# A GCN layer and a graph attention layer on one core: the turned data's write-outs on another queue, one fetch placed later, the attention products' PSUM banks exchanged

## The chip, the cores and the metric

The kernel runs on one core of a Trainium2 chip. The metric is the time of one execution in device microseconds, as the median of several runs; smaller is better. The kernel before has a median of 2262.29 us over three runs, from 2256.73 to 2267.03. One further execution was profiled; all times of single steps come from it.

## What is computed

The input x has 128 elements (b) of 128 nodes by 512 features, all float32, and one 128 by 128 adjacency matrix. Cut to what matters:

```
h = relu(layernorm(x));  x = x + norm_adj @ (h @ W0) + b0
h = relu(layernorm(x));  q, k, v = h @ Wq + bq, h @ Wk + bk, h @ Wv + bv     (8 heads of 64)
attn = softmax(q k^T / 8 + (1 - adj) * -1e9);  x = x + (attn @ v) @ Wo + bo
```

## The kernel before

**Groups and slots.** The 128 elements are 32 groups (NG) of four (GB). One pass of the outer loop, a slot t, works on three groups at once: the W block multiplies group t+1 by the GCN weight, the blocks Q, K and V make q, k and v of group t, and the Y block multiplies the attention output of group t-1 by Wo. Each of these five products is a fast (Strassen-like, seven products, with a second level inside) multiplication of seven steps, so the places in a slot are called W0 to W6, Q0 to Q6, K0 to K6, V0 to V6 and Y0 to Y6; a "b" or "c" behind a place is a point after the first or second part of that step.

**The order is written by hand.** `at(slot, place, f, ...)` puts a function into a table, and `block` calls what stands at a place before it issues that step's products. Every engine executes its instructions in the order in which these calls issue them, so a place decides the position in each engine's queue. All DMAs of the kernel before are issued by SyncE (SP) and stand in one queue; SyncE waits at the head of its queue until what the next DMA needs is there. Eight semaphores are given to the DMAs in turn, so that a DMA also waits until the one issued eight before it has landed.

**Turning data through DRAM.** The attention weights of an element (128 queries by 8 heads by 128 keys) have to be transposed before they can be multiplied by v. `flip_att(g, b)` transposes blocks of 32 by 32 on VectorE (L917) and writes the 512 KB to a scratch tensor in DRAM (`turned<-att`, L918); `turn_att(g, b)` fetches them from there with the blocks exchanged, in four DMAs of 128 KB whose runs are 128 bytes long (`att<-turned`, L789, through `from_dram`). The normalised input of the attention layer takes the same way: `flip_h` (L776) and its write (`turned_h`, L778), and `turn_h` with `op_h<-turned_h` (L789). The first and the last group transpose on TensorE instead, in whole or in part.

**Where these steps stand in a slot of the middle** (group g = t-1; a minus means the slot before):

| element | exponentials and softmax end | flip and write | fetch |
|---|---|---|---|
| 0 | V and Y block of the slot before | Y6c of the slot before | W3 |
| 1 | Y block of the slot before | Q0b | Q2b |
| 2 | Y block of the slot before | Q2c | K0 |
| 3 | Y5 of the slot before to W2 | Q4b | K0b |

**The products.** `attend(g, b)` at V0 multiplies the turned weights of element b by v: 16 products on TensorE (L943), then a copy of the result by ScalarE into the operand of the Wo product (L407). The order of the elements is 2, 0, 1, 3. Elements 2 and 3 use the two small PSUM banks (`po`), element 0 uses bank b, element 1 that one of the banks a0 and a1 which the last step of k has used. Right before, VectorE still adds up k from bank b and that bank a (L481, L496); right behind come the scores of the next group (L868, in the order 0, 1, 3, 2), those of element 1 into bank b and the same bank a.

**Weights.** The weights don't fit into SBUF together. Each product's combined weight (40 slots, five parts of eight) is fetched anew in every slot, in five DMAs of 512 KB (`reload_w`, L1133), as soon as the product before it in the same buffer has read its part. `reloads_of` lists the places: those under "Q" fetch v (into q's buffer), under "K" fetch o, under "V" fetch q, under "Y" fetch k. v's second part stands at Q6c, and the products that last read its place in the buffer are those of Q6.

**Other steps that count below.** ScalarE reads q and k from PSUM (L811, L814), takes the statistics of the group that comes in (L340, L341), normalises (L372) and copies the mixed operands (L407, `op_a<-pa`); GpSimd works out the scale from the statistics (L349 to L354).

Of the kernel before, what the change touches and what calls it, by code (L numbers as in the profile page):

```python
# [97 lines left out]
def kernel(  # L98
# [16 lines left out]
    nc = tc.nc  # L115
# [6 lines left out]
    NG = B // GB  # L122
# [21 lines left out]
    def small_bank(name):  # L144
        return ps_t.tile([P, 512], F32, tag="bank", name=name)
# [4 lines left out]
    bank = {k: ps_c.tile([P, 512], F32, tag=f"bank_{k}", name=f"bank_{k}") for k in ("a0", "a1", "d0", "d1", "b", "c")}  # L150
    turn = [0]
# [7 lines left out]
    att_dram = [dp.tile([P, H * P], F32, tag=f"turned_{b}", name=f"turned_{b}") for b in range(GB)]  # L159
    h_dram = [dp.tile([P, H * P], F32, tag=f"turned_h_{y}", name=f"turned_h_{y}") for y in range(2)]  # L160
# [609 lines left out]
    def flip_h(g, b):  # L770

        half, j = divmod(b, 2)
        h2 = hs.pop((g, b)).rearrange("n (c i f) -> n c i f", c=NC, i=4)
        t = op_att.t[:, SLOTS - 12 : SLOTS - 4, :] if half else att_of(g - 2, 2 if g > 2 else 1)
        t = t.rearrange("p s n -> p (s n)")
        nc.vector.transpose(t.rearrange("n (i c j f) -> n j c i f", i=4, c=NC, j=2)[:, j], h2)  # L776
        if j:
            nc.sync.dma_start(h_dram[half], t)  # L778

    def turn_h(g, half):  # L780
        op_h[g] = op_norm
        first = LEFT_AT[S1 if half else A11]
        from_dram(op_norm.t[:, first : first + 8, :], h_dram[half])
# [46 lines left out]

    maxima, sums = {}, {}

    def att_of(g, b):


        return att_buf[(b if g == 0 else b + 4 - 2 * g) % (GB + 1)]

    def by_blocks(g, b):  # L840

        return 0 < g < NG - 1 and not turned_in_place(g, b)

    def weights_of(g, b):

        return att_of(g, b - 1 if 0 < g < NG - 1 else b)

    def turned(g, b):

        if turned_in_place(g, b):  # L850
            return weights_of(g, b)
        return att_of(g, b - 2 if g else b - 1)

    def turned_in_place(g, b):

        return g == NG - 1 or g == 0 and b >= 2
# [55 lines left out]
    def flip_att(g, b):  # L912

        t = turned(g, b).rearrange("q h k -> q (h k)")
        order = "q h (i k) -> q h i k" if by_blocks(g, b) else "q h (k i) -> q h i k"
        dst = t.rearrange("q (i h k) -> q h i k", i=4, h=H)
        nc.vector.transpose(dst, weights_of(g, b).rearrange(order, i=4))  # L917
        nc.sync.dma_start(att_dram[b], t)  # L918

    def turn_att(g, b):  # L920
        from_dram(turned(g, b), att_dram[b])
# [10 lines left out]
    def attend(g, b):  # L932
        if g not in op_o:
            op_o[g] = op_norm if g == NG - 1 else op_att
        aT = turned(g, b)
        if b == 2 or b == 3:
            po = small_bank(f"po_{g}_{b}")
        else:
            po = bank["b" if b == 0 else f"a{1 - turn[0]}"]
        for c in range(NC):  # L940
            for p in range(2):
                h = 2 * c + p
                nc.tensor.matmul(  # L943
                    po[p * HD : (p + 1) * HD, c * P : (c + 1) * P],
                    vs[g][:, b, h * HD : (h + 1) * HD],
                    aT[:, p * NC + c, :],
                    start=True,
                    stop=True,
                )
        op_o[g].fill(nc.scalar.copy, b, po)  # L950
# [18 lines left out]
    def at(slot, place, f, *args):  # L969
        plan.setdefault((slot, place), []).append((f, *args))  # L970

    for t in range(-1, NG + 1):


        last = t == NG - 1
        if 0 <= t - 1 < NG - 1:
            g = t - 1

            for first, final, place, f, *args in (
                ("W4", "-Y6c", "W1c" if t == 2 else "-Y6c", flip_att, 0),  # L980
                ("W6", "Q2", "W4" if t == 2 else "W3", turn_att, 0),
                ("Q4c", "Q1c", "Q0b", flip_att, 1),
                ("Q6", "Q3", "Q2b", turn_att, 1),
                ("W6", "-Y3", "-Y3", exponentials, 2, 0, H // 2),
                ("Q3c", "-Y4", "-Y4", exponentials, 2, H // 2, H),
                ("Q6b", "-Y5b", "W0c" if t == 2 else "-Y5b", softmax_end, 2),
                ("K0c", "-Y5", "-Y5", exponentials, 3, 0, H // 2),
                ("K1c", "-Y6", "-Y6", exponentials, 3, H // 2, H),
                ("K3c", "W0", "W2", softmax_end, 3),
                ("K1", "Q2c", "Q2c", flip_att, 2),  # L990
                ("K3", "Q4", "K0", turn_att, 2),
                ("K3", "Q3c", "Q4b", flip_att, 3),
                ("K5", "Q5", "K0b", turn_att, 3),
            ):
                place = first if t == 1 else final if last else place
                if f in (flip_att, turn_att) and turned_in_place(g, args[0]):
                    continue
                at(t - place.startswith("-"), place.strip("-"), f, g, *args)
            if t == 1:
                at(1, "K4", transpose_att, g, 2)  # L1000
                at(1, "K6", transpose_att, g, 3)
            for b in (2, 0, 1, 3):
                at(t, "V0", attend, g, b)
        if t == 0:

            at(0, "Q0b", ln2, 1, 0)
            at(0, "Q1b", ln2, 1, 1)
            at(0, "K6", norm_h, 1, 0)
            at(0, "K6", norm_h, 1, 1)
            at(0, "V4", transpose_h, 1, 0)  # L1010
            at(0, "V4", norm_h, 1, 2)
            at(0, "V5", transpose_h, 1, 1)
            at(0, "V5", norm_h, 1, 3)
            at(1, "W0", transpose_h, 1, 2)
            at(1, "W1", transpose_h, 1, 3)
            at(1, "W1b", attention_operands, 1)
            at(2, "Q5", attention_residual, 1, 0)
            at(2, "K1", attention_residual, 1, 1)
        elif 1 <= t + 1 < NG and t >= 0:
            g = t + 1  # L1020
            at(t, "Q3b" if g < NG - 1 else "Q0b", ln2, g, 0)
            at(t, "K0b" if g < NG - 1 else "Q3b", ln2, g, 1)
            if g == NG - 1:

                places = ("Q3", "Q4", "Q5", "Q5", "Q6", "Q6", "K1", "K2", "K2")
                steps = ((norm_h, 0), (norm_h, 1), (transpose_h, 0), (norm_h, 2), (transpose_h, 1), (norm_h, 3))
                steps += ((transpose_h, 2), (transpose_h, 3))
            else:
                places = ("K1c", "K2c", "K4c", "K5b", "K3", "K4b", "K6b", "K6b", "Y6b")
                if t == 1:  # L1030
                    places = ("K2c", "K3c", "K6", "K6b", "K4b", "K5b", "V0b", "V0b", "Y6b")
                steps = ((norm_h, 0), (norm_h, 1), (norm_h, 2), (norm_h, 3))
                steps += tuple((flip_h, b) for b in range(GB))
                for half in range(2):
                    at(t, ("V3", "Y0")[half], turn_h, g, half)
            for place, (f, b) in zip(places, steps):
                at(t, place, f, g, b)
            at(t, places[8], attention_operands, g)
            at(t + 1, "Q3", attention_residual, g, 0)
            at(t + 1, "Q4", attention_residual, g, 1)  # L1040
# [3 lines left out]
        if 3 <= t + 2 < NG:  # L1044
            place = (t - 1, "Y6b") if t > 1 else (t, "W0")
            at(*place, load_x, t + 2, (0,), t > 1)
            at(*place, load_x, t + 2, (1,), t > 1)
        if 2 <= t + 2 < NG:
            g = t + 2
# [13 lines left out]
        if 0 <= t < NG:  # L1063
            g = t
# [30 lines left out]
        if last:  # L1095
            g = t
# [38 lines left out]
    def reloads_of(t):  # L1135

        when = {
            "Q": ((t, "Q2"), (t, "Q6c"), (t, "K1"), (t, "K1"), (t, "K3")),
            "K": ((t, "K5"), (t, "V0c"), (t, "V0c"), (t, "V0c"), (t, "V0c")),
            "V": ((t, "V3"), (t, "Y0"), (t, "Y0"), (t, "Y0"), (t, "Y3")),  # L1140
            "Y": ((t, "Y4"), (t + 1, "W2"), (t + 1, "W4"), (t + 1, "Q1"), (t + 1, "Q1")),
        }
        if t + 1 == NG - 1:

            when["Y"] = ((t, "V2"),) * len(PARTS)
        elif t == NG - 1:

            when["Q"] = ((t, "K3"),) * len(PARTS)
        if t == 1:

            when["Q"] = ((1, "K4"),) * len(PARTS)
            when["K"] = ((1, "V0c"),) * len(PARTS)
        for kind in "QKVY":
            if kind in "QKV" and t == NG:
                continue
            reading[0] += 1
            for part, place in enumerate(when[kind]):
                at(*place, reload_w, reading[0] + 2, part)
# [159 lines left out]
```

## Time and profile before

| quantity | value |
|---|---|
| median of three runs | 2262.29 us (2256.73 to 2267.03) |
| the profiled execution, its own time | 2243.55 us |
| its span, first to last instruction | 2241.8 us |
| TensorE busy | 2200.8 us, 98% of the span |
| VectorE, GpSimd, ScalarE busy | 1884.1, 1868.6, 1285.5 us |
| DMA: bytes moved, mean rate | 599.23 MB, 267 GB/s |
| packets under 512 bytes | 765664 of 908108 |
| `turned<-att`: DMAs, median time from issue to landing | 122 of 512 KB, 5.2 us |
| `att<-turned`: the same | 488 of 128 KB, 4.0 us |

How to read it: the busy share of an engine says how much of the span it has work; the view of waits says what an engine that had none was waiting for. The timeline gives, for each group of instructions, the start, the length, the engine, the line, what it writes and reads, the count, and in brackets the idle time before it with what ended it. SyncE's rows give the time in which it issues DMAs, not the transfers. A transfer's time from issue to landing is in the list of DMA issues and in the chain of waits. TensorE's products are pipelined: the next one starts before the one before has ended.

### The profile page before, as it was taken

The page shows a single profiled execution, that of the slowest core. Times are in us where ns is not written, and L with a number is a line of the kernel's source. Part 1 is how long each engine was busy: PE and PEld are TensorE (multiplying, and loading weights), DVE is VectorE, ACT ScalarE, POOL GpSimd, SP SyncE. Part 2 cuts the span into 40 slices and gives each one's busy share as a digit, 9 for nine tenths or more (in the row PEclk, how much of TensorE's full clock was granted, in tenths as well). Part 3 has the DMA queues.
Part 4 walks back from the last instruction along what each step waited for, and adds up shares of the span by engine and source line. Part 5 has one row for each costly group of instructions (what it writes and reads, how often), then busy time and mean ns, then how long its engine had stood idle before and what let it go on. Part 6 is the DMA issues. An engine that isn't in the chain of part 4 may idle for free.

```text
span 2241.8 us, 78690 instructions
## 1 busy us (share of the span) xinstructions
PE 2200.8 (98%) x31597; PEld 1877.0 (84%) x31597; DVE 1884.1 (84%) x4252; ACT 1285.5 (57%) x3813; POOL 1868.6 (83%) x1994
## 2 busy tenths in 40 slices
PE   9989999999999999999999999999999999999999
PEld 6777888888888888888888888888888888888887
DVE  7787888888888888888888878888888888888886
ACT  3566655656556556566565575655665655756444
POOL 6898888888888988889888888888898888898764
PEclk9999999999999999999999999999999999999999
DMA  5389999999999999999999999999999999999994
GB/s 162 142 259 274 276 292 272 252 279 273 297 283 284 262 263 293 257 298 262 286 268 294 272 249 293 266 301 272 284 272 291 268 295 283 271 282 284 259 251 173
DMA packets 908108, 599.23 MB, mean 267 GB/s; under 512 B 765664, under 2 KB 772960, under 8 KB 907104
## 3 DMA queue, kind: packets, MB, share of 16 engines
q1 hardware_dynamic: 907744, 594.20, 91.2%
q8 instruction: 250, 4.10, 0.8%
q14 instruction: 114, 0.93, 0.1%
HBM read 455.68 MB, written 138.41 MB: 265 GB/s over the span
## 4 chain that ended last, share of the span: by engine, by line
PE 81%; DVE 7%; DMA 6%; SPq 3%; issue 1%; POOL 1%; ACT 1%; DVEq 0%; POOLq 0%
PE bank_a L142 31%; PE bank_d L142 18%; PE bank_b L142 10%; PE bank_c L142 9%; PE pa L142 4%; SPq L789 3%; DVE k L481 3%; PE bank_d L868 3%; DMA turned<-att 3%; DMA att<-turned 2%; PE po L943 2%; DVE q L481 2%; PE pss L868 1%; PE bank_b L868 1%; PE bank_b L943 1%
## 5 line engine op out<-in xcount | busy, mean ns | idle before, releaser
L899 ACT ACTIVATE att<-att,nmx 128x128 f32<-128x128 f32 x1024 | 402.9, 506 | 2.2 <-DVE nmx L887 1.5
L910 POOL TENSOR_TENSOR att<-att,rsm 128x1024 f32<-128x1024 f32 x121 | 229.5, 1897 | 149.3 <-DVE rsm L904 124.5
L142 PE MATMUL bank_a<-op_h,w 128*64 128x256 f32 x2976 | 352.8, 379 | 0.0
L811 ACT ACTIVATE q<-bank_a,bqk 128x256 f32<-128x256 f32 x192 | 79.9, 466 | 438.7 <-PE bank_a L142 438.7
L481 DVE TENSOR_TENSOR xt<-xt,bank_d 128x512 f32<-128x512 f32 x610 | 270.6, 468 | 11.8 <-PE bank_d L142 0.8
L142 PEld LDWEIGHTS bank_a<-op_h,w 128*64 128x64 f32 x2976 | 207.5, 137 | 81.6 <-issue 0.2
L94 POOL TENSOR_TENSOR op_o<-op_o 128x256 f32<-128x256 f32 x297 | 213.9, 739 | 27.2 <-DVE v L481 10.2
L142 PE MATMUL bank_d<-op_h,w 128*64 128x128 f32 (+1 forms) x3424 | 221.7, 275 | 0.0
L899 ACT ACTIVATION_READ_ACCUMULATOR att<-att,nmx 128x1 f32 x1024 | 211.0, 206 | 0.0
L94 POOL TENSOR_TENSOR op_a<-op_a 128x256 f32<-128x256 f32 x279 | 197.9, 733 | 15.1 <-ACT v L825 5.4
L142 PEld LDWEIGHTS bank_d<-op_h,w 128*64 128x64 f32 x3424 | 195.1, 137 | 6.7 <-issue 0.2
L94 POOL TENSOR_TENSOR op_h<-op_h 128x256 f32<-128x256 f32 x270 | 191.0, 731 | 9.4
L372 ACT ACTIVATE h<-xt,nb,rs 128x512 f32<-128x512 f32 x142 | 173.3, 1226 | 16.9 <-POOL nb L357 15.2
L142 PE MATMUL bank_a<-w,op_o 128*64 128x256 f32 x1536 | 182.2, 379 | 0.0
L142 PE MATMUL bank_a<-w,op_h 128*64 128x256 f32 x1488 | 178.0, 381 | 0.0
L142 PE MATMUL bank_a<-w,op_a 128*64 128x256 f32 x1488 | 176.5, 379 | 0.0
L496 DVE TENSOR_TENSOR xt<-bank_a,xt 128x512 f32<-128x512 f32 x252 | 165.9, 679 | 2.8 <-PE bank_a L142 2.8
L825 ACT COPY v<-bank_a 128x512 f32<-128x512 f32 x96 | 56.2, 585 | 181.9 <-PE bank_a L142 143.4
L887 DVE TENSOR_REDUCE nmx<-att 128x8 f32<-128x1024 f32 x128 | 152.5, 1209 | 0.6 <-POOL att L883 0.6
L917 DVE STREAM_TRANSPOSE att<-att 128x1024 f32<-128x1024 f32 x122 | 152.5, 1250 | 0.3 <-ACT att L899 0.2
L875 DVE SCALAR_TENSOR_TENSOR att<-bank_d,msk 128x512 f32<-128x512 f32 x128 | 82.4, 685 | 82.8 <-PE bank_d L868 82.7
L377 POOL TENSOR_TENSOR xt<-xt,b_o 128x1024 f32<-128x1024 f32 x62 | 147.5, 2381 | 0.0
(198 smaller groups left out, 5851.1 us busy)
## 6 DMA issues: line engine op xcount, KB each, us to landing
w<-wd_v SPq DMA_DIRECT2D x155, 512.0 KB, 6.5
w<-wd_o SPq DMA_DIRECT2D x155, 512.0 KB, 9.9
w<-wd_q SPq DMA_DIRECT2D x150, 512.0 KB, 5.3
w<-wd_k SPq DMA_DIRECT2D x150, 512.0 KB, 7.6
turned<-att SPq DMA_DIRECT2D x122, 512.0 KB, 5.2
att<-turned SPq DMA_DIRECT2D x488, 128.0 KB, 4.0
out_dram<-xt SPq DMA_DIRECT2D x62, 512.0 KB, 5.0
op_h<-turned_h SPq DMA_DIRECT2D x232, 128.0 KB, 4.9
```

The costliest lines, as they stand in the source:

```text
L94: engine.tensor_tensor(twice(out), twice(x), twice(y), ALU.subtract if minus else ALU.add)
L142: nc.tensor.matmul(out[y : y + P // 2], lhsT[:, y : y + P // 2], rhs, **flags)
L372: nc.scalar.activation(dst, src, AF.Relu, bias=nb[:, j : j + 1], scale=rs[:, j : j + 1])
L377: engine.tensor_tensor(t, src, bias.unsqueeze(1).to_broadcast([P, t.shape[1], D]), ALU.add)
L481: nc.vector.tensor_tensor(dst, dst, src, f)
L496: nc.vector.tensor_tensor(t, src.rearrange("p (r f) -> p r f", r=2), t, ALU.add)
L868: nc.tensor.matmul(pss[p][:, c, :], qs[g][rows, c, cols], ks[g][rows, c, cols], start=True, stop=True)
L875: nc.vector.scalar_tensor_tensor(dst, pss[p], SCALE, mask, ALU.mult, ALU.add)
L887: nc.vector.tensor_reduce(nmx, att_of(g, b), AX.X, ALU.max, negate=True)
L899: nc.scalar.activation(dst, src, AF.Exp, bias=nmx[:, h : h + 1], scale=1.0, accum_out=sm[:, h : h + 1])
L910: engine.tensor_tensor(att, att, rsm.unsqueeze(2).to_broadcast([P, H, P]), ALU.mult)
L917: nc.vector.transpose(dst, weights_of(g, b).rearrange(order, i=4))
```

## The change

Three things. **First**, the writes of turned data (attention weights of the groups 1 to 29, normalised input from group 3 to 30) are issued by ScalarE's queue and no longer by SyncE's: 172 DMAs. The flips remember the tile in `turned_to_dram`, and `write_turned` issues the DMA at a place of its own: Y6c of the slot before, Q1, Q3c and Q5 for the elements 0 to 3, K5b and V0 for the two halves of the normalised input. The first and last groups keep theirs on SyncE. **Second**, the fetch of element 1 goes from Q2b to K0, behind v's second part (Q6c), so that the fetches of the elements 1, 2 and 3 follow one another, and some reloads get other places, which leaves them in the order v1, v2, the twelve fetches, v3, v4, v5, o1 on SyncE. **Third**, except in the last group, the elements 2 and 0 take the small banks, element 1 takes bank b and element 3 the bank a. The order of the elements stays 2, 0, 1, 3.

```
     def flip_h(g, b):
...
-        if j:
+        if j and g == 2:
             nc.sync.dma_start(h_dram[half], t)
+        elif j:
+            turned_to_dram["h", half] = t
+
+    def write_turned(kind, n):
+        dram = h_dram if kind == "h" else att_dram
+        nc.scalar.dma_start(dram[n], turned_to_dram.pop((kind, n)))
...
     def flip_att(g, b):
...
-        nc.sync.dma_start(att_dram[b], t)
+        if 0 < g < NG - 2:
+            turned_to_dram["att", b] = t
+        else:
+            nc.sync.dma_start(att_dram[b], t)
...
     def attend(g, b):
...
-        if b == 2 or b == 3:
+        if b in ((2, 3) if g == NG - 1 else (0, 2)):
             po = small_bank(f"po_{g}_{b}")
         else:
-            po = bank["b" if b == 0 else f"a{1 - turn[0]}"]
+            po = bank["b" if b == (0 if g == NG - 1 else 1) else f"a{1 - turn[0]}"]
...
-                ("Q6", "Q3", "Q2b", turn_att, 1),
+                ("Q6", "Q3", "K0", turn_att, 1),
...
+                if f == flip_att and 1 < t and not last:
+                    b = args[0]
+                    place = ("W3" if t == 2 else "-Y6c", "Q1", "Q3c", "Q5")[b]
+                    at(t - place.startswith("-"), place.strip("-"), write_turned, "att", b)
...
+            if 1 < t and g < NG - 1:
+                at(t, "K5b", write_turned, "h", 0)
+                at(t, "V0", write_turned, "h", 1)
...
-            "Q": ((t, "Q2"), (t, "Q6c"), (t, "K1"), (t, "K1"), (t, "K3")),
-            "K": ((t, "K5"), (t, "V0c"), (t, "V0c"), (t, "V0c"), (t, "V0c")),
+            "Q": ((t, "Q3c"), (t, "Q6c"), (t, "K5c"), (t, "K5c"), (t, "K5c")),
+            "K": ((t, "K5c"), (t, "V0c"), (t, "V0c"), (t, "V0c"), (t, "V0c")),
             "V": ((t, "V3"), (t, "Y0"), (t, "Y0"), (t, "Y0"), (t, "Y3")),
-            "Y": ((t, "Y4"), (t + 1, "W2"), (t + 1, "W4"), (t + 1, "Q1"), (t + 1, "Q1")),
+            "Y": ((t, "Y4"), (t + 1, "W2"), (t + 1, "W4"), (t + 1, "Q0c"), (t + 1, "Q1")),
```

More of the change, by code (lines that the diff above doesn't have):

```diff
@@ L827, in values @@
         return Projection(lambda: op_h[g], "v", region, False, first, g > 0).steps()
-    maxima, sums = {}, {}
+    maxima, sums, turned_to_dram = {}, {}, {}
     def att_of(g, b):
```

## The prediction, made before the changed kernel ran

> **What bounds the kernel now.** I read the page first, then the waits of TensorE, then its timeline around one slot, then SyncE's timeline in a quiet and in a late slot.
>
> ```profile
> span 2241.8 us, 78690 instructions
> PE 2200.8 (98%) x31597; PEld 1877.0 (84%) x31597; DVE 1884.1 (84%) x4252; ACT 1285.5 (57%) x3813; POOL 1868.6 (83%) x1994
> ```
>
> TensorE is the bound; all that this change can win is its 41 us of idle time, and time in which products are held apart by less than their modelled ends show. TensorE's waits, by who ended them (total, times, longest):
>
> ```profile
> PE po L943 <- DMA att<-turned: 16.9, 15, 3.4
> PE bank_b L943 <- DVE k L481: 4.4, 17, 0.3
> ```
>
> Both stand at V0, before the attention products. The timeline of TensorE there, in a slot without a late DMA:
>
> ```profile
> 1041.94 1.05 PE L943 MATMUL po<-att,v 128*64 128x128 f32 x16
> 1043.26 1.09 PE L943 MATMUL bank_b<-att,v 128*64 128x128 f32 x16 [0.27 <-DVE k L481]
> 1044.18 1.04 PE L943 MATMUL bank_a<-att,v 128*64 128x128 f32 x16
> 1045.06 1.04 PE L943 MATMUL po<-att,v 128*64 128x128 f32 x16
> 1046.03 1.16 PE L868 MATMUL bank_d<-k,q 64*128 64x128 f32 x16
> ```
>
> Sixteen products need 0.88 us (1044.18 to 1045.06). From the first to the second group are 1.32 us, so waiting for bank b costs 0.44 us, more than the 0.27 us of idle time; bank a costs another 0.04.
>
> The start of the scores (L868 on bank_d) marks the slots in the timeline. Of the 28 slots from 218.5 to 2136.8 us, 16 last 67.9 us, one 68.0, one 67.1, and ten between 68.6 and 71.2. The surplus over 67.9 is 17.7 us in all: this is what late fetches cost. The cause is in SyncE's timeline. A quiet slot:
>
> ```profile
> 1085.33 0.33 SPq L918 DMA_DIRECT2D turned<-att  x1
> 1085.71 1.54 SPq L1133 DMA_DIRECT2D w<-wd_k  x2
> 1087.35 0.42 SPq L1133 DMA_DIRECT2D w<-wd_v  x1
> 1091.95 4.24 SPq L789 DMA_DIRECT2D att<-turned  x4
> 1096.23 1.96 SPq L918 DMA_DIRECT2D turned<-att  x2
> 1098.29 0.71 SPq L1133 DMA_DIRECT2D w<-wd_v  x1
> 1100.41 8.57 SPq L789 DMA_DIRECT2D att<-turned  x8
> ```
>
> and the same part of the latest slot, and its beginning:
>
> ```profile
> 935.03 0.34 SPq L918 DMA_DIRECT2D turned<-att  x1
> 935.41 0.44 SPq L962 DMA_DIRECT2D out_dram<-xt  x1
> 936.26 0.33 SPq L1133 DMA_DIRECT2D w<-wd_k  x1
> 945.64 2.97 SPq L789 DMA_DIRECT2D att<-turned  x4
> ...
> 961.35 2.17 SPq L918 DMA_DIRECT2D turned<-att  x2
> 963.62 0.41 SPq L1133 DMA_DIRECT2D w<-wd_v  x1
> 965.92 6.85 SPq L789 DMA_DIRECT2D att<-turned  x8
> ```
>
> A write is queued behind the reloads, the fetch waits for its landing, and all that follows on SyncE waits for the fetch: 9 us at 936.6. The writes of the elements 2 and 3, flipped by 1026.4 (L917 at 1025.12 for 1.24; plus 67.9 it is 1094.3), go out only at 1096.2, because SyncE stands in element 1's fetch. So a lateness early in the slot is handed on to the last fetch. SyncE's own waits say so:
>
> ```profile
> SPq L789 <- DMA turned<-att: 286.4, 90, 9.0
> ```
>
> **The change, part by part** (times of the slot that starts at about 1003; add 67.9 for the quiet slot above).
>
> *Banks.* The second group now goes to a small bank, last emptied at 1034.5 (L407). The third wants bank b at 1043.7; VectorE's last read of it ends at 1043.2. The fourth wants bank a at 1044.6, its last read ends at 1044.0. All three are free in time: 0.44 + 0.04 = 0.48 us less, I take 0.45. Next in line are the scores of element 1, which reuse bank a: element 3's copy (0.58 us, 0.05 after its products) ends near 1046.25, and they want it at about 1046.5: covered by 0.2 us. If that fails, 0.1 to 0.3 us come back. 28 slots x 0.45 = 12.6 us.
>
> *Writes on ScalarE.* 172 issues, each 0.33 to 0.38 us on SyncE (sometimes to 1.5). No row shows one on ScalarE. Per slot: element 0's falls into an idle stretch of 14.34 us (before L811 at 1017.11), those for the normalised input into idle stretches of 1.50 and 2.28 us (before L407 at 1043.03 and L872 at 1049.01). The others stand between instructions without a gap: element 1's behind L341 at 1018.6, element 2's behind L372 at 1023.7, element 3's behind L341 at 1026.7. Behind these wait the statistics, GpSimd's nb (ready 1028.9), h (L372, 1028.91 to 1029.73) and with it the mixing product at 1029.93, which gets h just in time. So bounds: 0, if the queue issues the DMA while the activation ahead of it runs; 3 x 0.35 = 1.05 us a slot, 29 us in all, if each delays the chain. A gain below 0 is excluded: nothing is taken off ScalarE. I take 0: consecutive activations here start before the one ahead has ended (L340 at 1017.84, its predecessor ends at 1017.95), so the queue looks ahead, and the activations ahead last 0.63 to 0.82 us. The flips are over in time as well: 1017.4, 1023.3, 1026.4.
>
> *SyncE and the fetch of element 1.* SyncE loses the waits for the flips and for landings in the middle of the reloads. The fetch waits behind v's second part, which TensorE frees with Q6 (bank_b at 1027.12 for 0.39): 1027.5. At that time all writes are long issued. Then twelve fetches follow. Their rate: 0.81 us each (four in 3.24 us at 1079.51) up to 1.07 (eight in 8.57). From 1028.1 the last one is issued at 1037.0 to 1039.9, and lands 4.0 us later (median): 1041.0 to 1043.9. TensorE asks for element 3 at 1044.6. By the same rule the quiet slot before has its last landing at 1108.2 + 4.0 = 1112.2, and TensorE asks at 1113.0. So the margin goes from 0.8 to between 0.7 and 3.6 us. More matters that lateness before v2 is no longer handed on: in the quiet slot SyncE is done with v1 at 1087.8 and meets v2's release at 1095.4, so some 7 us of lateness end there. What is late next: the same twelve fetches when DMA is slow inside these 17 us. Of the 17.7 us I take 13.7 off and leave 4; bounds 0 and 17.7.
>
> The other moved reloads change places only among themselves, behind releases that stand (v1 after Q1's products, v3 to v5 behind the fetches as before).
>
> *A rule that speaks against it.* The DMA engines are busy for 0.95 to 0.99 of a slot in the windows view, in quiet and late slots alike. The Trainium skill, "DMA: Bandwidth & Descriptors", section "Issuing engines are not separate DMA queues", says that DMAs from several engines share the same 16 DMA engines and that issuing from more than one saves only issue time. By that alone the writes would win nothing and the sum would be the banks' 12.6 us. The same page, section "Queues, rings and completion order", says that each issuing engine has a ring of its own and that rings are served in turn, by which a write would pass the reloads; no run yet shows it.
>
> **Sum.** Against the profiled execution: 2243.6 - 12.6 - 13.7 + 0 = 2217.3 us. That execution is 18.7 us below the median of the runs, and below all three. No view says why; carried over in full it gives 2236. If it is more of the same late fetches, it goes too: at the least 2243.6 - 12.6 - 17.7 = 2213.
>
> **Rivals.**
>
> *Nothing from the writes.* For: the DMA share above; if it is the transfers' sum that is late and not their order, stalls stay. Only the banks' gain is left: 2262.3 - 12.6 = 2250, or 2262 if late fetches take that back too. Against: the late slot shows SyncE waiting 9 us, not transferring. Likewise *ScalarE pays*: 1.05 us x 28 = 29 us eat the gain of 26: 2265; at two issues that delay, 0.7 x 28 = 20 us: 2256.
>
> *Slower: the twelve fetches.* They now stand in one chain between Q6 and element 3's products, 17.1 us, and no earlier start can help them. Each slot in which the last lands late pays the difference. To lose all that is won (17.7 + 12.6 = 30 us over 28 slots, 1.08 us a slot) it has to land at 1045.7 on average, so the last issue comes at 1041.7, and a fetch takes 13.6 / 11 = 1.23 us. The eight take 0.86 (965.92) and 1.07, element 1's four 1.06 and 1.09 (956.95), all below it. At 1.3 us the last lands at 1046.4, 1.8 us late: 28 x 1.8 = 51, less 30: +21, 2283 us. For it speaks that single issues take up to 3.9 us, and that the normalised input's write now comes on a queue of its own into the end of the chain.
>
> **Numbers.** Forecast, 2220 to 2250 around 2236: 0.56. The median's surplus goes too, 2213 to 2220: 0.12. Nothing from the writes: 0.10, and ScalarE pays: 0.06, together 2250 to 2265. Slower by the fetches, 2274 and more: 0.16. Range 2212 to 2264. A change below 0.5% (11 us) can't be told from none by this measurement: faster 0.68, same 0.16, slower 0.16.
>
> **What would show it.** Right: slots of 67.4 to 67.5 us between the starts of the scores; 0.88 us between the four groups of L943; no wait of TensorE for VectorE there; fetch rows x12 on SyncE directly behind v's second part; SyncE's wait for the writes' landing mostly gone; ScalarE's h still ending before the mixing product. Wrong: waits of the attention products for the fetches in most slots (the chain), waits of the mixing product for h (ScalarE), or slots stretched as before at a DMA share near 1 (transfers).

## The result, and the profile after

The changed kernel is slower. Its median is 2277.72 us over four runs (2277.08 to 2285.28), against 2262.07 us for the kernel before (2256.73 to 2267.03). The ratio of the compared runs is 1.0091, with a 95% interval from 1.0069 to 1.0112; the two medians by themselves stand at 1.0069. The prediction was 2236 us, with a range from 2212 to 2264. The profiled execution took 2277.08 us and is like its timed runs, while that of before lies 18.5 us below this median; so every comparison below goes by ratios of timed runs, and the two profiles are compared slot by slot, not by their spans.

The head of the page:

```profile
span 2275.3 us, 78602 instructions
PE 2209.9 (97%) x31597; PEld 1886.5 (83%) x31597; DVE 1883.9 (83%) x4252; ACT 1286.1 (57%) x3813; POOL 1868.0 (82%) x1994
```

Every engine is as busy as before to within 0.5%. What grew is TensorE's idle time, from 41 to 65 us, and, with the same 31597 products, its busy time, by 9.1 us.

The longer busy time goes with the granted clock, the share of full speed that the trace records for TensorE. It is 0.50 in five stretches of 3.4 to 6.8 us between 426 and 1966 us, where the profile of before has none between 216.4 us and its end. Four of the five begin within 1 us of the end of a wait of 4.0, 3.0, 2.3 or 2.2 us for element 3's fetch (two more waits of 3.0 us have none behind them), and sixteen products right behind the longest took 1.97 us instead of 1.09. Over the timed runs the mean granted clock is 0.991 to 0.995, against a mean of 0.998 for the kernel before in the experiments below. From these shares I estimate that up to 10 of the 20 us lost are products slowed after such a wait, and not the wait itself; no run separates the two.

TensorE's waits (total us, times, longest):

```profile
PE bank_a L953 <- DMA att<-turned: 35.7, 22, 4.0
PE bank_a L953 <- DVE op_o L776: 6.8, 5, 1.7
PE po L953 <- DMA att<-turned: 3.5, 3, 1.6
```

The wait for VectorE on bank b is gone. In its place the fourth group of attention products, element 3's, waits for its fetch in 22 slots by this view, and starts at least 1.5 us behind the third in each of 27 slots of the middle. One such slot in TensorE's timeline:

```profile
632.65 1.92 PE L953 MATMUL po<-att,v 128*64 128x128 f32 x32
634.39 1.05 PE L953 MATMUL bank_b<-att,v 128*64 128x128 f32 x16
636.63 1.09 PE L953 MATMUL bank_a<-att,v 128*64 128x128 f32 x16 [1.18 <-DMA att<-turned]
637.65 1.16 PE L875 MATMUL bank_d<-k,q 64*128 64x128 f32 x16
```

The first two groups now share one row, since they run without a gap: three groups stand 0.87 us apart (634.39 - 632.65 = 1.74 for two). The bank exchange does what it was to do, and the fourth group gives it back: 2.24 us from 634.39 to 636.63, so 1.37 us too late. Over 27 slots of the middle the mean distance between the starts of the scores is 69.76 us, where the profile of before has 68.56; the shortest slot is 68.1, so every one of these slots is longer than the 67.4 us that the prediction expected.

Why the fetch is late can be read from SyncE's timeline of that slot and the busy share of the DMA engines beside it. Element 0's write is issued by ScalarE at 596.94; SyncE, which no longer waits for the flip, has issued the output's first half (L972) and k's second part (L1150) before:

```profile
595.45 0.38 SPq L972 DMA_DIRECT2D out_dram<-xt  x1
595.93 0.42 SPq L1150 DMA_DIRECT2D w<-wd_k  x1
603.38 2.67 SPq L796 DMA_DIRECT2D att<-turned  x4
606.14 0.90 SPq L972 DMA_DIRECT2D out_dram<-xt  x1
607.09 1.82 SPq L1150 DMA_DIRECT2D w<-wd_k  x3
609.77 8.79 SPq L1150 DMA_DIRECT2D w<-wd_v  x2
619.55 12.96 SPq L796 DMA_DIRECT2D att<-turned  x12
```

The windows view, in steps of 2.5 us from the write's issue on (the last two columns are the busy share of the DMA engines and GB/s):

```profile
596.94:599.44 2.50, 2.50 (x50) 2.50 (x48) 2.12 (x6) 0.00 (x0) 2.42 (x3) 1.00 1.03 393
599.44:601.94 2.50, 2.50 (x34) 1.92 (x32) 2.46 (x7) 0.00 (x0) 2.34 (x3) 1.00 0.96 389
601.94:604.44 2.50, 2.50 (x38) 2.07 (x36) 2.36 (x7) 0.00 (x0) 2.42 (x4) 1.00 0.10 38
604.44:606.94 2.50, 2.50 (x36) 2.00 (x34) 2.50 (x7) 0.00 (x0) 2.42 (x5) 1.00 0.79 125
```

The write, the output and the weights run together for 5 us, and then **the DMA engines stand idle for 2.2 us** (a share of 0.10). SyncE is waiting for the write's landing before it may issue element 0's fetch (603.38), and nothing else is left that it could have issued. My reading is that in a slot in which these engines are otherwise busy throughout, that gap is handed on to the last of the twelve fetches. This rests on one slot so far; the experiments below test it.

The DMA issues (count, size, median us from issue to landing) show how long the writes take to land:

```profile
turned<-att ACTq DMA_DIRECT2D x116, 512.0 KB, 7.1
...
turned_h<-att ACTq DMA_DIRECT2D x28, 512.0 KB, 4.3
turned_h<-op_o ACTq DMA_DIRECT2D x28, 512.0 KB, 7.7
```

The attention writes took 5.2 us on SyncE's queue before and take 7.1 now. Not all of that comes from the queue: in the kernels below that have the new order and keep all writes on SyncE they take 6.3 and 6.8. The first half's write of the normalised input lands after 4.3 us instead of 8.2. This comes with the new order, since it lands after 4.1 and 4.2 us also where it stays on SyncE in that order.

### The profile page after: what moved, and what is told of

Read it like the earlier page. It is cut to its first block, busy times and chain, and to the rows that moved or that the text cites. A ratio compares the mean times of both kernels' runs of the same rounds, so it can differ in the third digit from the quotient of the medians.

```text
span 2275.3 us, 78602 instructions
## 1 busy us (share of the span) xinstructions
PE 2209.9 (97%) x31597; PEld 1886.5 (83%) x31597; DVE 1883.9 (83%) x4252; ACT 1286.1 (57%) x3813; POOL 1868.0 (82%) x1994
## 4 chain that ended last, share of the span: by engine, by line
PE 83%; DMA 7%; DVE 4%; SPq 3%; issue 1%; POOL 1%; ACT 1%; DVEq 0%; ACTq 0%; POOLq 0%
PE bank_a L142 32%; PE bank_d L142 19%; PE bank_b L142 10%; PE bank_c L142 9%; DMA att<-turned 5%; PE pa L142 5%; PE bank_d L875 3%; SPq L796 3%; DVE k L481 2%; PE bank_a L953 2%; PE pss L875 1%; PE bank_b L875 1%; DVE q L481 1%; DMA wd_o<-op_o 1%; DVE att L776 0%
## 5 line engine op out<-in xcount | busy, mean ns | idle before, releaser
L372 ACT ACTIVATE h<-xt,nb,rs 128x512 f32<-128x512 f32 x142 | 173.9, 1230 | 60.5 <-DMA att<-turned 28.9
L924 DVE STREAM_TRANSPOSE att<-att 128x1024 f32<-128x1024 f32 x122 | 152.5, 1250 | 0.3 <-ACT att L906 0.2
```

The costliest lines, as they stand in the source:

```text
L372: nc.scalar.activation(dst, src, AF.Relu, bias=nb[:, j : j + 1], scale=rs[:, j : j + 1])
```

## The experiments

All ratios are to the kernel before on the same chip, with 95% intervals. The chips differ by up to 0.5%, so ratios are compared and not times.

### One part alone

The bank exchange alone, in the kernel before:

```
-        if b == 2 or b == 3:
+        if b in ((2, 3) if g == NG - 1 else (0, 2)):
```

> The kernel before with only the banks of the attention products exchanged. All theories: the 0.44 us between the first two groups of products goes and the slots without a late fetch last 67.45 instead of 67.9 us. If the fetches' landing, not the banks, sets the end of the attention products in most slots, less of it is kept. Expected ratio 0.995 (about 12 us less), bounds 0.990 to 1.000; a ratio above 1.003 would mean that the exchange itself is the loss.

Measured: 1.0004 (0.9989 to 1.0019), at the end of the bounds and not the 0.995 expected. The shortest slots fall from 67.9 to 67.4 us, by the 0.45 predicted. But the mean slot is 69.1 us, and its waits say why:

```profile
PE po L943 <- DMA att<-turned: 20.7, 12, 3.2
PE bank_a L943 <- DMA att<-turned: 10.7, 13, 1.7
```

These 31.4 us stood at 16.9 in the profile of before, itself a low one: asking 0.45 us earlier for a fetch that comes when it comes wins nothing, if I read this rightly.

The writes alone on ScalarE's queue, with the order of the fetches and reloads as before:

> The kernel before with only the writes of turned data on ScalarE's queue, at the places of the change; the fetch of element 1, the reloads and the banks are those of before. Theory F (the loss is the order of the fetches: twelve in one row behind v's second part): ratio 0.990 to 1.000, since the queue of SyncE loses waits. Theory W (the loss is the writes: served in turn with the reloads they make both land late, or they hold ScalarE up): ratio 1.007 to 1.015, with stretched slots like those of the changed kernel.

Measured: 1.0164 (1.0142 to 1.0186). The worst of all, and the wait is another one:

```profile
PE pa L142 <- ACT h L372: 43.7, 30, 3.5
```

With element 1's fetch still at Q2b, element 2's write on ScalarE must wait until the DMA that used its semaphore before has landed: in 21 of 29 slots ScalarE stands idle ahead of it (32 us in all), and the write goes out 0.08 us after the landing of a reload of k. The activations behind it wait too, up to h and the mixing product. In the changed kernel there is no such slot.

The order of the fetches and reloads alone, all writes on SyncE, banks as before:

```
-                ("Q6", "Q3", "Q2b", turn_att, 1),
+                ("Q6", "Q3", "K0", turn_att, 1),
...
-            "Q": ((t, "Q2"), (t, "Q6c"), (t, "K1"), (t, "K1"), (t, "K3")),
+            "Q": ((t, "Q3c"), (t, "Q6c"), (t, "K5c"), (t, "K5c"), (t, "K5c")),
```

> The kernel before with only the places of the fetch of element 1 and of the reloads of the change; all writes stay on SyncE, banks as before. Theory F: slower, ratio 1.007 to 1.03, with waits of the attention products for the fetches in most slots. Theory W: within 0.995 to 1.005.

Measured: 0.9956 (0.9940 to 0.9972), against Theory F. The chain of twelve fetches, which the slower rival of the prediction blamed, comes with a gain. Order and banks together, all writes on SyncE:

> The kernel before with the change's order of fetches and reloads and its banks, all writes on SyncE: the change without its first part. Both theories: not slower than the order alone (0.9956); with the banks' 0.44 us a slot in the slots where no fetch is late 0.990 to 0.996.

Measured: 0.9976 (0.9963 to 0.9988). The expected further gain of the banks did not come; the interval overlaps that of the order alone. So **the writes on ScalarE turn a gain of 0.2 to 0.4% into a loss of 0.9%.**

The changed kernel with element 1's fetch and v's first part back in their old places:

```
-                ("Q6", "Q3", "K0", turn_att, 1),
+                ("Q6", "Q3", "Q2b", turn_att, 1),
...
-            "Q": ((t, "Q3c"), ...
+            "Q": ((t, "Q2"), ...
```

> The changed kernel with element 1's fetch at Q2b again, ahead of v's second part (v's first part at Q2); writes on ScalarE and banks exchanged as changed. Theory F: the loss is undone and the gains of the other two parts show, ratio to the kernel before 0.980 to 0.995. Theory W: it stays slow, 1.003 to 1.015.

Measured: 1.0137 (1.0108 to 1.0166), with 52.2 us of TensorE's waits for h, as in the run with the writes alone; here too element 2's write goes out on the landing of a reload of k in 22 of 29 slots. So the moved fetch is not the loss; that it helps is likely, but the interval just touches that of the changed kernel.

### Which of the writes

The changed kernel with the first half's normalised-input write moved from K5b to V0, still on ScalarE:

> The changed kernel with one move: the write of the normalised input's first half is issued by ScalarE at V0, behind the attention products, and no longer at K5b. Theory H (that write, on a ring of its own, is served between the last fetches of element 3 and makes the last one land over 1 us later, in every slot): the last fetch lands 3.8 to 4.0 us after its issue and no longer 5.2, most of TensorE's 39 us of waits for the fetches goes, ratio to the kernel before 0.985 to 0.995. Theory S (writes on a second ring slow the fetches and reloads altogether, whichever write it is): unchanged, 1.005 to 1.012.

Measured: 1.0067 (1.0048 to 1.0085), in Theory S's range and not in Theory H's. The last fetch lands 3.8 us after its issue again, as Theory H said, but the loss stays in large part, and GpSimd's op_o and VectorE now come late as well:

```profile
PE bank_c L142 <- DVE v L481: 10.9, 23, 0.9
PE bank_a L953 <- DMA att<-turned: 7.4, 8, 1.8
PE bank_b L142 <- POOL op_o L94: 6.2, 12, 1.0
```

Both normalised-input writes back on SyncE, the four attention writes on ScalarE:

> The changed kernel with both writes of the normalised input on SyncE again, where the flips are (behind the fetches in the queue); the attention weights' writes stay on ScalarE. Theory H: like the run with the late write, 0.985 to 0.997. Theory S: 1.003 to 1.012, since four of six writes a slot stay on the second ring.

Measured: 0.9990 (0.9979 to 1.0002), between the two theories. The reverse, only these two on ScalarE:

> The change with only the normalised input's writes on ScalarE (K5b and V0); the attention weights' writes on SyncE. Theory H: these writes carry the loss, so this is slower than the same kernel with all writes on SyncE by 0.5 to 1.3 us a slot, ratio to the kernel before 1.000 to 1.010, with the last fetch landing 5 us after its issue. Theory S: a third of the loss at most, ratio below 0.999.

Measured: 0.9962 (0.9951 to 0.9974): Theory H is refuted, for the last fetch does land 5.2 us after its issue here and nothing is lost. Only the second half's on ScalarE:

> Order and banks of the change, and of all writes only that of the normalised input's second half (V0) on ScalarE. If the first half's write in the end of the fetches costs 1.3 us there, as the time of the last fetch from issue to landing says (5.1 against 3.8 us), then this beats both halves on ScalarE (0.9962): 0.990 to 0.995. If it doesn't, 0.996 to 0.999.

Measured: 0.9964 (0.9950 to 0.9977), so the first half's write costs nothing there. The changed kernel with nothing but **element 0's write** back on SyncE:

```
-        if 0 < g < NG - 2:
+        if 0 < g < NG - 2 and b > 0:
             turned_to_dram["att", b] = t
```

> The changed kernel with only element 0's write of attention weights back on SyncE, at its flip; the other three and both halves of the normalised input stay on ScalarE. Theory P (a write on SyncE held the transfers behind it back until it was issued; on ScalarE, element 0's write is served in turn with a store and a reload that SyncE had already issued, lands 2 us later and with it everything up to the last fetch): ratio to the kernel before 0.995 to 1.000, like the run with only the normalised input's writes on ScalarE (0.9962). Theory S (five writes on the second ring are nearly as bad as six): 1.004 to 1.009.

Measured: 0.9946 (0.9928 to 0.9964), just below Theory P's range and far from Theory S's. Taking back one write of six undoes the whole loss. TensorE's waits for fetches fall from 39.2 to 12.0 us:

```profile
PE bank_a L953 <- DMA att<-turned: 9.8, 11, 2.0
...
PE po L953 <- DMA att<-turned: 2.2, 1, 2.2
```

and among SyncE's waits there is again the one for the flip (L924), while that for the writes' landing is halved from the 234.1 us that it has in the changed kernel:

```profile
SPq L796 <- DMA turned<-att: 111.9, 34, 7.1
SPq L928 <- DVE att L924: 86.1, 30, 6.9
```

Element 0's and the first half's write back on SyncE, the other four on ScalarE:

> The changed kernel with element 0's write and the first half's write of the normalised input back on SyncE; elements 1 to 3 and the second half stay on ScalarE. Theory P, with the collision at the end of the fetches as its second part: both losses are gone, 0.990 to 0.997. Theory S (four writes on the second ring): 1.000 to 1.005.

Measured: 0.9952 (0.9933 to 0.9970). And only these two on ScalarE, the other four on SyncE:

> The order of fetches and reloads and the banks as in the changed kernel, but of the six writes of a slot only element 0's and that of the normalised input's first half on ScalarE; four on SyncE. Theory of two writes (together they make the last fetch late, the other four do nothing): 1.005 to 1.012 of before. Rival (any write taken off SyncE adds its share): about a third of the changed kernel's surplus over the kernel with all writes on SyncE, 0.998 to 1.003.

Measured: 1.0114 (1.0093 to 1.0136): the two together are enough for the whole loss; neither alone is (0.9990 with element 0's among the four, 0.9962 with the first half's).

### Order or queue

If the two transfers ahead of element 0's write are the trouble, they can be moved behind its fetch:

```
-            "Y": ((t, "Y4"), (t + 1, "W2"), ...
+            "Y": ((t, "Y4"), (t + 1, "W4"), ...
...
+            elif 0 < t < NG - 2:
+                at(t + 1, "W3", store_half, t - 1, 0)
             elif 0 < t < NG:
                 store_half(t - 1, 0)
```

> The changed kernel, all writes on ScalarE, but the store of the finished group's first half and k's second part are placed behind element 0's fetch, so that SyncE has neither of them issued when element 0's write goes out. Theory P: the write lands about 5 us after its issue and no longer 7, the fetch of element 0 starts 2 us earlier, ratio 0.995 to 1.002. Theory S: 1.004 to 1.010.

Measured: 1.0127 (1.0097 to 1.0156): the loss stays, though the write lands after 5.1 us again. My theory of then, that the late landing by itself is what costs, falls with this. The windows from the write's issue (595.10) on:

```profile
595.10:597.60 2.50, 2.50 (x50) 2.50 (x48) 2.13 (x6) 0.00 (x0) 2.42 (x3) 1.00 0.94 370
597.60:600.10 2.50, 2.50 (x34) 1.92 (x32) 2.47 (x7) 0.00 (x0) 2.34 (x3) 1.00 0.06 16
600.10:602.60 2.50, 2.50 (x38) 2.07 (x36) 2.36 (x7) 0.00 (x0) 2.42 (x4) 1.00 0.85 133
```

Now the write is alone, and the same gap (a share of 0.06) comes right behind it. The gap is the round from the write to its fetch: transfer, landing, SyncE's wake-up, issue, first packets. What counts is whether something is **behind** the write and ahead of the fetch to fill it. Two runs put that to the test. In the first, the 512 KB stay on ScalarE's queue, but SyncE is held at the flip by a DMA of 512 bytes:

```
             turned_to_dram["att", b] = t
+            if b == 0:
+                nc.sync.dma_start(hold_dram, t[0:1, 0:P])
```

> The changed kernel with one more DMA a slot: SyncE writes 512 bytes of element 0's flipped tile to a scratch tensor nobody reads, at the place where it issued element 0's whole write before. So SyncE waits again for that flip before it issues the output's first half and k's second part, while the 512 KB still go out on ScalarE's queue. Theory L (what costs is that the output and k's second part are issued ahead of element 0's write): as with the write on SyncE, 0.993 to 0.999 of before. Theory R (the write on a queue of its own is what costs): as the changed kernel, 1.006 to 1.012.

Measured: 0.9971 (0.9955 to 0.9987). SyncE's timeline and the windows from the write on:

```profile
588.62 0.25 SPq L929 DMA_DIRECT2D hold<-att  x1
588.93 0.39 SPq L975 DMA_DIRECT2D out_dram<-xt  x1
589.41 0.50 SPq L1153 DMA_DIRECT2D w<-wd_k  x1
593.06 4.65 SPq L797 DMA_DIRECT2D att<-turned  x4
```

```profile
588.62:591.12 2.50, 2.50 (x50) 2.50 (x48) 2.13 (x6) 0.00 (x0) 2.42 (x3) 1.00 1.05 411
591.12:593.62 2.50, 2.50 (x34) 1.92 (x32) 2.47 (x7) 0.00 (x0) 2.34 (x3) 1.00 1.03 329
593.62:596.12 2.50, 2.50 (x38) 2.07 (x36) 2.36 (x7) 0.00 (x0) 2.42 (x4) 1.00 1.00 222
```

The output and k's part now come behind the write. The fetch is issued 4.4 us after it, not 6.4, and the three windows have no gap. The earlier fetch by itself is not what counts: on average of 27 slots it follows the write by 5.6 us here and 7.3 in the changed kernel, but by 7.2 also in the kernel with order and banks, which loses nothing. An added DMA has made the kernel 1.2% faster. In the second, element 0's write is on SyncE's own queue, but behind those two transfers:

```
-        nc.scalar.dma_start(dram[n], turned_to_dram.pop((kind, n)))
+        (nc.sync if (kind, n) == ("att", 0) else nc.scalar).dma_start(dram[n], ...)
...
-            "Y": ((t, "Y4"), (t + 1, "W2"), ...
+            "Y": ((t, "Y4"), (t + 1, "W0"), ...
```

with the write's place moved to W0b.

> The changed kernel with element 0's write on SyncE, but queued behind the output's first half and k's second part; the other writes on ScalarE. Theory L (order of these three is what costs): 1.005 to 1.012 of before, as the changed kernel, with the write landing some 7 us after its issue. Theory R (a queue of its own is what costs): 0.993 to 0.997, as with the write on SyncE ahead of the two.

Measured: 1.0145 (1.0119 to 1.0171), above Theory L's range and far from Theory R's. SyncE's timeline, and the windows from 599.13 on:

```profile
597.64 0.38 SPq L972 DMA_DIRECT2D out_dram<-xt  x1
598.12 0.42 SPq L1150 DMA_DIRECT2D w<-wd_k  x1
599.13 0.50 SPq L785 DMA_DIRECT2D turned<-att  x1
605.62 2.66 SPq L796 DMA_DIRECT2D att<-turned  x4
```

```profile
601.63:604.13 2.50, 2.50 (x34) 1.92 (x32) 2.47 (x7) 0.00 (x0) 2.34 (x3) 1.00 0.96 383
604.13:606.63 2.50, 2.50 (x38) 2.07 (x36) 2.36 (x7) 0.00 (x0) 2.42 (x4) 1.00 0.11 39
```

The same gap, 6.5 us from write to fetch, a loss no smaller, and no second queue for this write. So it is the order of three transfers and not the queue of element 0's write, given that the first half's write is on ScalarE as in both of these kernels.

### All kernels by one quantity

From the trace's packet times I worked out, for 24 slots of the middle of each kernel, how long the DMA engines are idle in the 12 us after the issue of element 0's write (one minus their busy share, in steps of 2 us, summed; other slots, or another way of summing, shift a row by up to 0.4 us and leave the two groups apart), and when the output's first half is issued against that write:

| kernel | ratio | idle, us a slot | output against the write |
|---|---|---|---|
| element 0's write back on SyncE | 0.9946 | 0.86 | 0.4 us behind |
| elements 1 to 3 and second half on ScalarE | 0.9952 | 0.95 | 0.4 behind |
| order alone | 0.9956 | 0.83 | |
| normalised-input writes on ScalarE | 0.9962 | 0.88 | 0.4 behind |
| second half's write on ScalarE | 0.9964 | 0.74 | |
| SyncE held | 0.9971 | 1.11 | 0.3 behind |
| order and banks | 0.9976 | 0.72 | 0.4 behind |
| normalised-input writes on SyncE | 0.9990 | 1.26 | 1.5 ahead |
| before | 1 | 0.88 | 0.4 behind |
| banks alone | 1.0004 | 0.90 | |
| first half's write at V0 | 1.0067 | 2.06 | 1.5 ahead |
| **changed kernel** | 1.0091 | 2.60 | 1.5 ahead |
| element 0's and first half's on ScalarE | 1.0114 | 2.40 | 1.5 ahead |
| output and k behind the fetch | 1.0127 | 3.32 | some 8 behind |
| element 1's fetch back | 1.0137 | 2.45 | 1.5 ahead |
| write behind output and k on SyncE | 1.0145 | 2.97 | 1.5 ahead |
| writes alone | 1.0164 | 3.10 | 1.5 ahead |

Every kernel at 1.0004 and below has at most 1.26 us of idle time there, every slower one at least 2.06. Between the changed kernel and the one with element 0's write on SyncE lie 1.74 us a slot, 47 us over 27 slots, of which 0.0145 x 2246 = 33 us reach the end.

How the gap reaches the end can be read from the same packets. The first of the twelve fetches is issued 50.0 us after the start of the scores in the kernel with element 0's write on SyncE and 50.1 us after it in the changed kernel, for v's second part waits there for TensorE in both. But up to that point the DMA engines have moved 15.15 MB in the one and 14.59 MB in the other (means of 27 slots). So 3.45 and 3.97 MB are left to move until the last of the twelve has landed, which is 67.0 and 68.5 us after the start of the scores. In the three other kernels with element 1's fetch at K0 that lose more than 1% (1.0114, 1.0127, 1.0145), 14.40 to 14.63 MB have been moved by then; in the seven with the new order at 0.9976 and below, 15.06 to 15.15.

The row that looks out of line explains the second write. With the normalised-input writes on SyncE the output is also issued ahead of element 0's write, yet the gap stays small: there the queue runs later, the output lands 8.4 us after the write's issue (6.3 in the changed kernel), behind the write's own landing (7.7), and so still fills the gap. With the first half's write on ScalarE, that write goes out some 2 us earlier in the slot, and what follows on SyncE comes forward by some 1.8 us; only then has it run empty. That both writes are needed is shown by the runs; this way in which the second one acts is read from the traces and has no run of its own.

## Why the prediction was wrong

**Banks: right in mechanism, worth nothing.** In the run with the banks alone the four groups stand 0.87 us apart in the slots without a late fetch, and these slots fell to 67.4 us as predicted; no product waits for VectorE on bank b. The term was still wrong, 12.6 us against 0 (1.0004): in a slot whose end is set by a fetch, an earlier request only waits longer. The prediction named this ("2262 if late fetches take that back too") and gave it too little weight.

**Writes on ScalarE: the price of the issues was right.** ScalarE's timeline beside element 3's write in the changed kernel:

```profile
617.45 0.72 ACT L341 ACTIVATE unused<-op_o,mv 128x512 uint8<-128x512 f32 x1
617.51 0.33 ACTq L785 DMA_DIRECT2D turned<-att  x1
618.08 0.19 ACT L341 ACTIVATION_READ_ACCUMULATOR unused<-op_o,mv 128x1 f32 x1
```

The issue takes 0.33 us and lies wholly inside the activation ahead of it. ScalarE does wait for landings ahead of h (28.9 us, 15 times), but TensorE's waits for h total 2.2 us. The rival "ScalarE pays" did not happen in this order; it did in the two kernels that kept element 1's fetch at Q2b, where ScalarE waited not for the issue but for a landing.

**The step that failed: "SyncE loses the waits for the flips"**, booked as part of the 13.7 us of gain. The wait for element 0's flip was what kept the output and k's second part behind the write; without it they run ahead, and, once the first half's write is off SyncE too, the round from the write to its fetch lies open. That is what lies between 0.9976, the same kernel with all writes on SyncE, and 1.0091. Holding SyncE again (0.9971) and reversing the order on SyncE's own queue (1.0145) show it from both sides. The working counted every instruction that moved by its own place and did not ask which instructions behind a removed wait would now be early.

**"Lateness before v2 is no longer handed on": right for SyncE's queue, wrong for the DMA engines.** SyncE does start the twelve fetches at the same point of the slot in the changed kernel as in the fastest one. But what the DMA engines have not moved in the gap is still to be moved then (some 0.5 MB), and that crosses v2. The order alone gains 0.44%, 10 us, where the term took 13.7. What it assumed for the chain was too short. Twelve fetches between 1028.1 and a last landing at 1041.0 to 1043.9 are 13 to 16 us; in the changed kernel they take 18.4 on average, 13.2 to issue and 5.2 to land, and in the kernel with order and banks 16.8. Their rate, 1.08 us, is just past the slow edge of the rows used. The 5.2 us instead of 3.8 come with the first half's write on ScalarE, which is issued beside the last two fetches; the runs with about 5 us that lose nothing (0.9946, 0.9962) show that it is no loss by itself.

**The rule that spoke against it.** Element 0's write lands on average 7.3 us after its issue on ScalarE's queue beside the output and k's second part (the changed kernel), and 8.0 us after it behind the same two on SyncE's (the kernel at 1.0145); the output lands 6.3 and 5.5 us after that issue. The Trainium skill, "DMA: Bandwidth & Descriptors", section "Issuing engines are not separate DMA queues", says that such DMAs share the engines whatever issued them and that only issue time is saved: the sharing agrees with these rows. That the rest of the change would then be neutral does not follow: what an issuing engine no longer waits for reorders all that it issues next.

**The slower rival** had the place right (the last fetch before element 3's products, and the normalised input's write in the end of the chain), and its cause wrong: the chain of twelve comes with a gain.

**What stays open.** The gain of the order alone is not split further, and why the loss per us of idle time differs between kernels (the changed one at 2.60 us loses less than others at 2.40) was not tried; the granted clock differs too, from 0.991 to 0.998 between the slower kernels, and was not separated. The best versions, from 0.9946 to 0.9964, can't be told apart by these intervals; all beat both kernels, most simply the order alone or the changed kernel with element 0's write left on SyncE.

## What to carry to other kernels

A wait on an issuing queue also orders what stands behind it: before taking it away, list what will be issued early, and what that was covering. Where a transfer has to land before the next may be issued, the DMA engines have a gap of that round; put independent transfers behind the first, neither ahead of it nor behind the second (0.9971 against 1.0145 and 1.0127 here). And when DMA engines are busy nearly all of a slot, look for their few idle windows first: a share of 0.10 for 2.5 us said more here than all the totals.

## What the runs showed of the hardware

The round from a 512 KB write to the first packets of its own fetch leaves the DMA engines idle for about 2.2 us, if nothing else is in flight (shares of 0.06, 0.10 and 0.11 in three kernels). A DMA issued on ScalarE's queue can pass one queued on SyncE's: the first half's write, issued in the changed kernel behind the last or the last but one fetch, lands ahead of the fetch issued before it in 26 of 28 slots, most often by 0.2 to 0.6 us. The last fetch then lands 5.2 us after its issue and not 3.8. And a DMA of 512 bytes, issued only for its wait, brought the changed kernel from 1.0091 to 0.9971.
